# Local attention with whitening: second moments in two column halves, and every row point of the first image through the common path

## The chip, the core and the metric

The kernel runs on one core of one Trainium2 chip. The metric is device time in microseconds (us) of one execution. Engines are called PE (the matmul array), DVE (vector), ACT (scalar), POOL (GpSimd) and SP (the queue that issues most DMAs).

## What is computed

`x` has 4 images of 256 channels and 64 x 64 pixels. Layer 0 makes 49 attention weights per pixel and sums the 49 shifted neighbours with them; layer 1 whitens the result in groups of 64 channels. Cut to what matters:

```python
# layer 0
k = conv(x, w1, padding=6, dilation=2) + b1      # 7 x 7, 256 -> 128 channels
k = conv1x1(k, w2) + b2                          # 128 -> 49
attn = softmax(k, axis=1)
out = sum over (u, v) in 7 x 7 of attn[7u+v] * shift(x, 2u, 2v)
# layer 1, for every group g of 64 channels, m = 4*64*64 pixels
xc = X - mean(X)
Sigma = 1e-5 * I + xc @ xc.T / m                 # 64 x 64 per group
P = five Newton steps towards Sigma^(-1/2), Sigma scaled by its trace
y = (P / sqrt(trace)) @ xc * weight + bias
```

Only the 64 x 64 blocks of second moments within a group are used, never those between groups.

## The kernel before

Everything is fp32. The 256 channels lie as two chunks (`NCC`, index `cc`) of 128 partitions; a chunk holds two channel groups of 64 (`GW`). Each image is kept as two slots, one for each row parity, and dilation 2 makes each parity of rows and columns a plain 7 x 7 problem.

**Weight products (lines 198 to 236).** The two convolutions are folded into one with 49 outputs: for each of the 49 taps and each chunk the tap's slice of `w1` is the stationary side (`w1_sb[cc][:, :, tap]`, a column step of 49 words), and `w2` is the moving side. The 7-tap convolution is evaluated at seven points (0, 1, -1, 2, -2, 1/2 and infinity, `EVAL`, with `INF` = 6), so the moving side `w2c` holds `w2` scaled for the points. Four taps (`s` = 0) or three (`s` = 1) accumulate in one PSUM tile, which ACT copies to `gr` (the five middle points), `gr0` (point 0) and `gr6` (infinity). The latter two live in `lgx`, which later holds the logits of images 1 to 3.

**Row points (lines 275 to 440, helpers `add`, `sub`, `madd` at 262 to 270).** An image goes through row points `br`, and each through three banks of column points (`BANKS`). `row_eval` combines four input rows into `rb`; for points 0 and infinity it is only two ACT copies. `weights` combines the products for a bank into `wr` tiles the first time and writes them to DRAM (`gd`); later images read them back over SP. `col_eval` makes the column points `xh` on DVE. `conv_bank` multiplies into PSUM `cv`, 49 columns in each half of the array for the two column parities; ACT copies to `pv`; `col_interp` and, after the last row point, `row_interp` turn points back into pixels on DVE. `conv_step(k, i)` issues the matmuls of row point k, bank i, and then prepares the same bank of row point k+1. The first image takes only five row points this way (`MID`); points 0 and infinity are computed by `direct` (line 508) from `x` itself with single tap columns: 84 products into PSUM tile `acc`, placed after row points 1, 2 and 3.

**Attention (lines 601 to 731).** `softmax` of one column parity (`pc`) and one half of the rows turns logits, normalises and writes weights to DRAM (`sd`, 4 DMAs a call for each row parity). `load_band` reads a diagonal band back into the one tile `band`, DVE transposes it (line 666), and `weighted_sum` multiplies it with turned pixels into PSUM `y` (line 712). There are four such quarter images for each image (`n` = 0 to 15), each as `first_half` and `second_half`. ACT stores `y` over the input slot.

**Second moments (lines 736 to 763).** `turn_y` transposes a piece of the result, ACT copies it to `yt` (3 buffers, set to 1 beforehand, so that the last column of each chunk stays 1 and gives the sums), and `moments` adds 128 x 129 products for both chunks to PSUM `sig`, eight pieces for each quarter. Pieces 4 to 7 are done in `finish`, when the next quarter begins.

**Order of the work.** PE keeps the program's order. While row points of image b+1 are computed, pieces of image b's attention are called in eight gaps of that loop: `plan(b, j, ...)` puts work in gap j of image b, gaps from 8 on going to the next image. The softmax of an image takes gaps 0 and 1 of the next. Images 0 and 1 have their halves from gap 2 on, two at a time; images 2 and 3 have one half in each gap from gap 3 on. What is left over after the last convolution runs in a tail. After it `finish`, the 64 x 64 Newton steps (lines 899 to 962) and the output.

Of the kernel before, what the change touches and what calls it, by code (L numbers as in the profile page):

```python
# [30 lines left out]
def kernel(  # L31
# [134 lines left out]
    for k in range(2):  # L166
        t = ps_cv.tile([P, 512], F32, name=f"cv{k}")
        nc.vector.memset(t, 0.0)
        cv_buf.append(t)
    sig = ps_sg.tile([P, NCC, P + 1], F32, name="sig")  # L170

# [9 lines left out]
    w2c = w1p.tile([O1, 4, NP, KT], F32, name="w2c")  # L181

    def load_w1(cc):
        nc.sync.dma_start(
# [2 lines left out]
        )  # L187

    load_w1(0)
    load_w1(1)  # L190
    load_x(0, 0, nc.sync)
    load_x(1, 1, nc.sync)
    for cc in range(NCC):
        cs = slice(cc * P, (cc + 1) * P)
        nc.sync.dma_start(gain_sb[:, cc : cc + 1], gain[0, cs].rearrange("c a b -> c (a b)"))
        nc.sync.dma_start(shift_sb[:, cc : cc + 1], shift[0, cs].rearrange("c a b -> c (a b)"))

    WCOL = (INF,) + tuple(range(1, NP - 1)) + (0,)
    for a in range(4):
        for k, b in enumerate(WCOL):  # L200
            f = EVAL[b][a] * SCALE[b]
            if f:
                nc.vector.tensor_scalar(w2c[:, a, k], w2T[:, :KT], f, None, ALU.mult)
            elif (a, b) == (0, INF):
                nc.vector.memset(w2c[:, a, k], 0.0)


    n0, n6 = KS * NCC * 2 * KT, KS * NCC * KT
    lgx = const.tile([P, max(SH * W, n0 + n6)], F32, name="lgx")
    gr0 = lgx[:, :n0].rearrange("p (v a s k) -> p v a s k", v=KS, a=NCC, s=2)  # L210
    gr6 = lgx[:, n0 : n0 + n6].rearrange("p (v a k) -> p v a k", v=KS, a=NCC)

    for cc in range(NCC):
        for v in range(KS):
            for s in range(2):
                t = tp()
                na = min(4, KS - 4 * s)
                for a in range(na):
                    k0 = 0 if a == 3 or (a == 0 and s == 0) else 1
                    k1 = NP if a == 0 else NP - 1  # L220
                    pe(
                        nc.tensor.matmul(  # L222
                            t[:, k0 * KT : k1 * KT],
                            w1_sb[cc][:, :, (KS - 1 - 4 * s - a) * KS + v],
                            w2c[:, a, k0:k1].rearrange("p b k -> p (b k)"),
                            start=(a == 0), stop=(a == na - 1),
                        )
                    )
                nc.scalar.copy(
                    gr[:, :, v, cc, s],  # L230
                    t[:, KT : (NP - 1) * KT].rearrange("p (b k) -> p b k", b=MID),
                )
                nc.scalar.copy(gr0[:, v, cc, s], t[:, (NP - 1) * KT : NP * KT])
                if s == 0:
                    nc.scalar.copy(gr6[:, v, cc], t[:, :KT])
    w1p.release()

    s24 = ctx.enter_context(tc.tile_pool(name="s24", bufs=1, reuse_waits="tile"))
# [31 lines left out]
        return STT(o, a, f, b, ALU.mult, ALU.add)  # L270


    made = set()

    def weights(b, br, i):

        first = (br, i) not in made
        made.add((br, i))
        w = {}
        for bc in BANKS[i]:
            w[bc] = apool.tile(
                [P, len(taps(bc)), nsk[br]], F32, tag="wr", name=f"wr_{b}_{br}_{bc}", bufs=7
            )
            if not first:
                nc.sync.dma_start(w[bc], gd[br][:, slot_of[bc] : slot_of[bc] + len(taps(bc))])
        if not first:  # L290
            return w

        if br == INF:
# [186 lines left out]
    def row_interp(b):  # L480

        pt = {k: zz[:K2, k] for k in range(NP)}
        lg = lgx
        if b == 0:
            lg = store[4].rearrange("p c r w -> p (c r w)")
        lg = lg[:, : SH * W].rearrange("p (r w) -> p r w", w=W)
# [4 lines left out]
        logits[b] = lg  # L491

    logits = {}

    def direct(br, s):


        a = 3 if br == INF else 0
        if s == 0:
            acc[0] = ps_y.tile([P, 2, Q8, W], F32, tag="y", name=f"acc{br}")  # L500
            nc.vector.memset(acc[0], 0.0)  # L501
        ps = acc[0][:, s]
        order = [(v, cc) for v in sorted(range(KS), key=lambda v: abs(v - R)) for cc in range(NCC)]
        for j, (v, cc) in enumerate(order):
            d = 2 * (v - R)
            w0, w1_ = max(0, -d), min(W, W - d)
            for h in range(2):
                xs = slots[h].rearrange("p c (q a) w -> p a q c w", a=4)
                pe(
                    nc.tensor.matmul(  # L510
                        ps[h * HB : h * HB + KT, :, w0:w1_],
                        gr6[:, v, cc] if br == INF else gr0[:, v, cc, s],
                        xs[:, a, :, cc, w0 + d : w1_ + d],
                        start=(j == 0),
                        stop=(j == len(order) - 1),
                        skip_group_check=True,
                    )
                )
        z = zz[:K2, br]
        if s == 0:  # L520
            nc.scalar.copy(z[:, :Q8], ps[:K2])
            if br == INF:
                nc.vector.memset(z[:, Q8], 0.0)
        else:
            nc.scalar.copy(z[:, Q8], ps[:K2, Q8 - 1])
            add(z[:, 1:Q8], z[:, 1:Q8], ps[:K2, : Q8 - 1])

    acc = [None]
    rows = [(0, br) for br in ROWS if br not in (0, INF)]
    rows += [(b, br) for b in range(1, B) for br in ROWS]  # L530
    cur, nxt = {}, {}

    def prepare(k, i):
# [19 lines left out]
                row_interp(b)  # L553


    for k in range(MID):
        for i in range(len(BANKS)):
            conv_step(k, i)
        if 1 <= k < 4:
            direct(*((INF, 0), (0, 0), (0, 1))[k - 1])  # L560
        if k == 1:
            for s in range(2, 4):
                load_x(s, s, nc.gpsimd)
    gpool.release()

# [16 lines left out]
    NY = 3  # L582
    yt_buf = []
    for k in range(NY):
        a = bpool.tile([P, NCC, P + 1], F32, name=f"yt{k}")
        nc.gpsimd.memset(a, 1.0)
        yt_buf.append(a)
    sd = []
# [11 lines left out]

    def softmax(b, pc, hf):

        lv = logits[b].rearrange("p r w -> p (r w)")
        lt = tp().rearrange("p (i h k) -> p i h k", i=NI, h=2)
        for i in range(NI):
            pe(
# [129 lines left out]
    def turn_y(n, i):  # L736
        yt, pc = where(n)
        t = tp()
        for cc in range(NCC):
            pe(  # L740
                nc.tensor.transpose(  # L741
                    t[:, cc * P : (cc + 1) * P],
                    yt[:, cc, CR * i : CR * (i + 1), bass.ds(pc, SW, 2)],
                    ident,
                )
            )
        yb = ybs[n, i] = yt_buf[len(ybs) % NY]
        nc.scalar.copy(yb[:, :, :P], t[:, :C].rearrange("p (a c) -> p a c", a=NCC))  # L748

    def moments(n, i):  # L750
        yb = ybs[n, i]
        for cc in range(NCC):
            pe(
                nc.tensor.matmul(  # L754
                    sig[:, cc],
                    yb[:, cc, :P],
                    yb[:, cc, :],
                    start=(count[0] == 0 and cc == 0),
                    stop=(count[0] == 4 * B * NCH - 1),
                    skip_group_check=True,  # L760
                )
            )
        count[0] += 1

    spill = {}
# [87 lines left out]
    for b in range(B):  # L853
        hs = [
            (lambda n=n, f=f: f(n))
            for n in range(4 * b, 4 * b + 4)
            for f in (first_half, second_half)
        ]
        if b + 2 < B:

            plan(b + 1, 2, *hs[:2])
            plan(b + 1, 3, *hs[2:4])
            plan(b + 1, 4, finish)
            for j in range(4):
                plan(b + 1, 5 + j, hs[4 + j])
        else:
            for j in range(8):
                plan(b + 1, 3 + j, hs[j])
    for b in range(B):
        for j in range(2):  # L870
            plan(b + 1, j, lambda b=b, j=j: soft(b, j))
    plan(1, 1, lambda: load_x(4, 4, nc.gpsimd))

    def gap(b, j):
        for f in todo.pop((b, j), ()):
# [2 lines left out]
    for b in range(1, B):  # L878
        j = 0
        for q in range(nb):  # L880
            conv_step(MID + NP * (b - 1) + q // len(BANKS), q % len(BANKS))
            if (q + 1) * NPC >= (j + 1) * nb:
                gap(b, j)
                j += 1
# [15 lines left out]
    for cc in range(NCC):  # L900
        G = sig[:, cc]
        mu = work.tile([P, 1], F32, tag="mu", name=f"mu{cc}")
        nc.vector.tensor_scalar(mu, G[:, P : P + 1], 1.0 / NPIX, None, ALU.mult)
# [124 lines left out]
```

## Time and profile before

| | us |
|---|---|
| runs of the kernel | 983.78, 984.85, 984.92; median 984.85 |
| profiled execution, own time | 984.85 |
| its span, first to last instruction | 983.1 |
| busy PE, PE weight loads, DVE, ACT, POOL | 786.6, 666.2, 640.7, 298.3, 38.1 |
| weight products | 12.1 to 61.7 |
| first image up to the first weighted sum | 61.7 to 267.7 |
| rest of the loops, to the last convolution | 267.7 to 711.4 |
| tail with image 3's attention | 711.4 to 881.6 |
| Newton steps, then output | 881.6 to 920.5, to 983.1 |

The page of a profile gives busy time for each engine, the span in 40 slices with the busy tenths of each, the chain of work that ended last, and groups of instructions by line: count, busy time, mean duration of one in ns, the idle time of the engine just before them and what ended it. A group's busy time is a union, so overlapping matmuls count once. PE's own row and its weight loads (PEld) are separate; every fp32 product appears as two records of each. A duration contains latency: how fast a run of equal instructions goes is read from start to start in the timeline. A tile name stands for all of its buffers.

### The profile page before, as it was taken

The page shows a single profiled execution, that of the slowest core. Times are in us where ns is not written, and L with a number is a line of the kernel's source. Part 1 is how long each engine was busy: PE and PEld are TensorE (multiplying, and loading weights), DVE is VectorE, ACT ScalarE, POOL GpSimd, SP SyncE. Part 2 cuts the span into 40 slices and gives each one's busy share as a digit, 9 for nine tenths or more (in the row PEclk, how much of TensorE's full clock was granted, in tenths as well). Part 3 has the DMA queues.
Part 4 walks back from the last instruction along what each step waited for, and adds up shares of the span by engine and source line. Part 5 has one row for each costly group of instructions (what it writes and reads, how often), then busy time and mean ns, then how long its engine had stood idle before and what let it go on. Part 6 is the DMA issues. An engine that isn't in the chain of part 4 may idle for free.

```text
span 983.1 us, 18542 instructions
## 1 busy us (share of the span) xinstructions
PE 786.6 (80%) x7511; PEld 666.2 (68%) x7511; DVE 640.7 (65%) x1414; ACT 298.3 (30%) x677; POOL 38.1 (4%) x50
## 2 busy tenths in 40 slices
PE   5969829916699998958999896699983678786898
PEld 4968606816598897957898796598972557663443
DVE  2249997797968859994996799995572111113344
ACT  1333222321133343422434342133341323330143
POOL 2120001200000100010010000000000000000000
PEclk9989959958799999988999998799986979995699
DMA  8944111607762822598183239623219712100277
GB/s 303 203 102 149 55 53 55 232 29 159 146 129 60 246 67 67 168 198 165 39 242 97 53 88 163 146 55 77 61 63 268 131 42 48 44 1 0 88 309 287
DMA packets 187693, 120.10 MB, mean 122 GB/s; under 512 B 139303, under 2 KB 178648, under 8 KB 186584
## 3 DMA queue, kind: packets, MB, share of 16 engines
q1 hardware_dynamic: 182584, 88.77, 36.2%
q0 software_dynamic: 5024, 30.15, 10.0%
q8 instruction: 59, 0.97, 0.4%
q14 instruction: 26, 0.21, 0.1%
HBM read 67.68 MB, written 51.21 MB: 121 GB/s over the span
## 4 chain that ended last, share of the span: by engine, by line
PE 54%; DVE 16%; SPq 5%; DMA 4%; ACT 3%; issue 3%; DVEq 0%; ACTq 0%
PE cv L422 19%; PE y L712 15%; PE tp L974 6%; SPq L643 5%; PE sig L754 4%; PE acc L510 2%; PE tp L680 2%; DVE pv L270 2%; PE tp L741 2%; DMA band<-sd 2%; DVE xh L270 2%; DMA sd<-zt 2%; DVE band L666 1%; ACT slot L726 1%; DVE ct L270 1%
## 5 line engine op out<-in xcount | busy, mean ns | idle before, releaser
L422 PE MATMUL cv<-xh,wr 128*49 128x128 f32 (+1 forms) x5096 | 310.1, 284 | 31.0 <-issue 15.5
L422 PEld LDWEIGHTS cv<-xh,wr 128*49 128x49 f32 x5096 | 300.5, 126 | 39.1 <-issue 26.9
L712 PE MATMUL y<-band,xb 128*128 128x352 f32 (+5 forms) x768 | 177.9, 374 | 67.0 <-DVE band L666 53.9
L712 PEld LDWEIGHTS y<-band,xb 128*128 128x128 f32 x768 | 124.0, 205 | 87.5 <-issue 57.7
L666 DVE STREAM_TRANSPOSE band<-band 128x1408 f32<-128x1408 f32 x32 | 50.6, 1619 | 84.7 <-DMA band<-sd 84.7
L754 PE MATMUL sig<-yt 128*128 128x129 f32 x512 | 82.3, 283 | 16.5 <-ACT yt L748 16.5
L687 ACT COPY xb<-tp 128x256 f32<-128x256 f32 x128 | 45.7, 373 | 140.5 <-PE tp L680 140.3
L754 PEld LDWEIGHTS sig<-yt 128*128 128x128 f32 x512 | 71.2, 195 | 22.7 <-ACT yt L748 19.9
L431 ACT COPY pv<-cv 113x486 f32<-113x486 f32 (+1 forms) x78 | 36.7, 473 | 111.0 <-PE cv L422 110.8
L741 PE MATMUL tp<-ident,slot 128*128 128x128 f32 x256 | 53.5, 301 | 10.7 <-ACT slot L726 9.8
L726 ACT ACTIVATE slot<-y,pivot 128x512 f32<-128x512 f32 x64 | 42.5, 719 | 61.5 <-PE y L712 61.5
L748 ACT COPY yt<-tp 128x256 f32<-128x256 f32 x128 | 45.1, 376 | 34.2 <-PE tp L741 33.7
L222 PE MATMUL tp<-w2c,w 128*128 128x245 f32 (+2 forms) x196 | 49.6, 418 | 7.2 <-DMA w<-in_L_conv_w_dram 7.2
L222 PEld LDWEIGHTS tp<-w2c,w 128*128 128x128 f32 x196 | 47.8, 306 | 8.8 <-issue 8.2
L270 DVE SCALAR_TENSOR_TENSOR xh<-ct 128x512 f32<-128x512 f32 x52 | 34.1, 684 | 28.5 <-PE cv L422 28.5
L680 PEld LDWEIGHTS tp<-ident,slot 128*128 128x128 f32 x256 | 43.9, 204 | 12.5 <-issue 6.8
L510 PE MATMUL acc<-slot,lgx 128*49 128x496 f32 (+3 forms) x168 | 36.0, 587 | 20.2 <-DVE acc L501 20.2
L741 PEld LDWEIGHTS tp<-ident,slot 128*128 128x128 f32 x256 | 39.6, 204 | 18.5 <-ACT slot L726 15.1
L680 PE MATMUL tp<-ident,slot 128*128 128x128 f32 x256 | 51.8, 298 | 0.0
L989 DVE TENSOR_SCALAR out<-tp,scale,beta 128x512 f32<-128x512 f32 x32 | 25.9, 809 | 32.4 <-PE tp L974 32.4
L270 DVE SCALAR_TENSOR_TENSOR pv<-pv 113x162 f32<-113x162 f32 x156 | 45.6, 319 | 0.1
L270 DVE SCALAR_TENSOR_TENSOR xh<-rb 128x512 f32<-128x512 f32 x26 | 17.8, 686 | 35.4 <-PE cv L422 35.4
(166 smaller groups left out, 893.0 us busy)
## 6 DMA issues: line engine op xcount, KB each, us to landing
wr<-gd SPq DMA_DIRECT2D x102, 196.0 KB, 2.8
out_dram<-out SPq DMA_DIRECT2D x32, 512.0 KB, 2.6
sd<-zt SPq DMA_DIRECT2D x128, 112.0 KB, 3.0
band<-sd SPq DMA_DIRECT2D x64, 224.0 KB, 4.3
slot<-in_x_dram POOLq DMA_DIRECT2D x12, 1024.0 KB, 10.4
gd<-wr SPq DMA_DIRECT2D x36, 196.0 KB, 2.1
w<-in_L_conv_w_dram SPq DMA_DIRECT2D x2, 3136.0 KB, 15.0
spill<-slot POOLq DMA_DIRECT2D x3, 2048.0 KB, 9.5
```

The source lines that it names most:

```text
L222: nc.tensor.matmul(t[:, k0 * KT : k1 * KT], w1_sb[cc][:, :, (KS - 1 - 4 * s - a) * KS + v], w2c[:, a, k0:k1].rearrange("p b k -> p (b k)") ...
L270: return STT(o, a, f, b, ALU.mult, ALU.add)
L422: nc.tensor.matmul(cv[h * HB : h * HB + KT, k, sr : sr + n, sc : sc + n], wv[:, sc, sr, cc], xh[bc][:, :n, h * NCC + cc, :n], start=(j == ...
L510: nc.tensor.matmul(ps[h * HB : h * HB + KT, :, w0:w1_], gr6[:, v, cc] if br == INF else gr0[:, v, cc, s], xs[:, a, :, cc, w0 + d : w1_ + d ...
L643: nc.sync.dma_start(bass.AP(tensor=D.tensor, offset=D.offset + CR * (NI * hf + i) * DR + (KS - 1) * SW, ap=[[DQ, P], [DR - SW, KS], [1, SW ...
L666: nc.vector.transpose(f, f)
L680: nc.tensor.transpose(t[:, cc * P : (cc + 1) * P], xt[:, cc, CR * m : CR * (m + 1), bass.ds(pc, SW, 2)], ident,)
L712: nc.tensor.matmul(ps[:, cc, q0 - half * HALF : q1 - half * HALF, :], xb[:, cc * P : (cc + 1) * P], rhs, start=(k == 0), stop=(k == len(PI ...
L726: nc.scalar.activation(yt[:, cc, half * HALF : (half + 1) * HALF, bass.ds(pc, SW, 2)], ps[:, cc], AF.Identity, bias=pivot[:, cc : cc + 1],)
L741: nc.tensor.transpose(t[:, cc * P : (cc + 1) * P], yt[:, cc, CR * i : CR * (i + 1), bass.ds(pc, SW, 2)], ident,)
L754: nc.tensor.matmul(sig[:, cc], yb[:, cc, :P], yb[:, cc, :], start=(count[0] == 0 and cc == 0), stop=(count[0] == 4 * B * NCH - 1), skip_gr ...
L974: nc.tensor.matmul(t, wm[cc], slots[2 * b + pr][:, cc, q * TR : (q + 1) * TR, :].rearrange("p r w -> p (r w)"), start=True, stop=True,)
```

## The change

- `sig` shrinks from 129 to 65 columns for each chunk. `moments` issues, for each chunk, one product for each channel group: 64 stationary columns, 65 moving ones (64 channels and the ones), into the group's 64 partitions of `sig`, that is, into one half of the array's columns. `yt` has a ones column after each 64 channels.
- The Newton part clears `S` and scales the two diagonal blocks into it.
- `direct` is gone. The first image takes all seven row points in the common order (infinity, 0, 1, -1, 2, -2, 1/2), and its logits go to `lgx` like those of the others, so slot 4 is free from the beginning and is loaded with slots 2 and 3.
- Weight products: the five middle points (`middle`, 245 moving columns) and the end points (`ends`, single taps with `w2`, 49 moving columns, seven of them in one PSUM tile and one ACT copy) are separate, in the order ends, middle, ends, middle. `x`'s first slot is loaded ahead of the second chunk of `w1`.
- Halves of images 2 and 3 are planned from gap 2 instead of gap 3.

```diff
-    sig = ps_sg.tile([P, NCC, P + 1], F32, name="sig")
+    sig = ps_sg.tile([P, NCC, GW + 1], F32, name="sig")
...
     load_w1(0)
+    load_x(0, 0, nc.sync)
     load_w1(1)
-    load_x(0, 0, nc.sync)
     load_x(1, 1, nc.sync)
...
+    def tap(cc, a, s, v):
+        return w1_sb[cc][:, :, (KS - 1 - 4 * s - a) * KS + v]
+
+    def ends(cc):
+        for dst, a, s in ((gr6[:, :, cc], 3, 0), (gr0[:, :, cc, 0], 0, 0), (gr0[:, :, cc, 1], 0, 1)):
+            t = tp()
+            for v in range(KS):
+                pe(
+                    nc.tensor.matmul(
+                        t[:, v * KT : (v + 1) * KT], tap(cc, a, s, v), w2T[:, :KT],
+                        start=True, stop=True,
+                    )
+                )
+            nc.scalar.copy(dst, t[:, : KS * KT].rearrange("p (v k) -> p v k", v=KS))
...
-                    k0 = 0 if a == 3 or (a == 0 and s == 0) else 1
-                    k1 = NP if a == 0 else NP - 1
                     pe(
                         nc.tensor.matmul(
-                            t[:, k0 * KT : k1 * KT],
-                            w1_sb[cc][:, :, (KS - 1 - 4 * s - a) * KS + v],
-                            w2c[:, a, k0:k1].rearrange("p b k -> p (b k)"),
+                            t[:, : MID * KT], tap(cc, a, s, v),
+                            w2c[:, a].rearrange("p b k -> p (b k)"),
                             start=(a == 0), stop=(a == na - 1),
                         )
                     )
...
-                nc.scalar.copy(gr0[:, v, cc, s], t[:, (NP - 1) * KT : NP * KT])
-                if s == 0:
-                    nc.scalar.copy(gr6[:, v, cc], t[:, :KT])
+    ends(0)
+    middle(0)
+    ends(1)
+    middle(1)
...
-    rows = [(0, br) for br in ROWS if br not in (0, INF)]
-    rows += [(b, br) for b in range(1, B) for br in ROWS]
+    rows = [(b, br) for b in range(B) for br in ROWS]
...
-    for k in range(MID):
+    for k in range(NP):
         for i in range(len(BANKS)):
             conv_step(k, i)
-        if 1 <= k < 4:
-            direct(*((INF, 0), (0, 0), (0, 1))[k - 1])
         if k == 1:
-            for s in range(2, 4):
+            for s in range(2, 5):
                 load_x(s, s, nc.gpsimd)
...
-        a = bpool.tile([P, NCC, P + 1], F32, name=f"yt{k}")
+        a = bpool.tile([P, NCC, P // GW, GW + 1], F32, name=f"yt{k}")
...
-            pe(
-                nc.tensor.matmul(
-                    sig[:, cc],
-                    yb[:, cc, :P],
-                    yb[:, cc, :],
-                    start=(count[0] == 0 and cc == 0),
-                    stop=(count[0] == 4 * B * NCH - 1),
-                    skip_group_check=True,
+            for g in range(P // GW):
+                pe(
+                    nc.tensor.matmul(
+                        sig[g * GW : (g + 1) * GW, cc],
+                        yb[:, cc, g, :GW],
+                        yb[:, cc, g],
+                        start=(count[0] == 0 and cc == 0),
+                        stop=(count[0] == 4 * B * NCH - 1),
+                        skip_group_check=True,
+                    )
                 )
-            )
...
-                plan(b + 1, 3 + j, hs[j])
+                plan(b + 1, 2 + j, hs[j])
...
-    plan(1, 1, lambda: load_x(4, 4, nc.gpsimd))
...
-        nc.vector.tensor_scalar(S, G[:, :P], 1.0 / NPIX, None, ALU.mult)
+        nc.vector.memset(S, 0.0)
+        for g in range(P // GW):
+            gs = slice(g * GW, (g + 1) * GW)
+            nc.vector.tensor_scalar(S[gs, gs], G[gs, :GW], 1.0 / NPIX, None, ALU.mult)
```

More of the change, by code (lines that the diff above doesn't have):

```diff
@@ L180 @@
     w1_sb = [w1p.tile([O1, P, KT], F32, name=f"w1_{cc}") for cc in range(NCC)]
-    w2c = w1p.tile([O1, 4, NP, KT], F32, name="w2c")
+    w2c = w1p.tile([O1, 4, MID, KT], F32, name="w2c")
     def load_w1(cc):
@@ L196, with middle @@
         nc.sync.dma_start(shift_sb[:, cc : cc + 1], shift[0, cs].rearrange("c a b -> c (a b)"))
-    WCOL = (INF,) + tuple(range(1, NP - 1)) + (0,)
     for a in range(4):
[L200 to L205, printed above, removed]
+        for b in range(1, NP - 1):
+            nc.vector.tensor_scalar(
+                w2c[:, a, b - 1], w2T[:, :KT], EVAL[b][a] * SCALE[b], None, ALU.mult
+            )
     n0, n6 = KS * NCC * 2 * KT, KS * NCC * KT
     lgx = const.tile([P, max(SH * W, n0 + n6)], F32, name="lgx")
+    lg = lgx[:, : SH * W].rearrange("p (r w) -> p r w", w=W)
     gr0 = lgx[:, :n0].rearrange("p (v a s k) -> p v a s k", v=KS, a=NCC, s=2)
     gr6 = lgx[:, n0 : n0 + n6].rearrange("p (v a k) -> p v a k", v=KS, a=NCC)
-    for cc in range(NCC):
+    def tap(cc, a, s, v):
[11 more added lines that the diff above has]
+            nc.scalar.copy(dst, t[:, : KS * KT].rearrange("p (v k) -> p v k", v=KS))
+    def middle(cc):
         for v in range(KS):
@@ L230 @@
                     gr[:, :, v, cc, s],
-                    t[:, KT : (NP - 1) * KT].rearrange("p (b k) -> p b k", b=MID),
+                    t[:, : MID * KT].rearrange("p (b k) -> p b k", b=MID),
                 )
-                nc.scalar.copy(gr0[:, v, cc, s], t[:, (NP - 1) * KT : NP * KT])
-                if s == 0:
-                    nc.scalar.copy(gr6[:, v, cc], t[:, :KT])
+    ends(0)
+    middle(0)
+    ends(1)
+    middle(1)
     w1p.release()
@@ L270, in madd @@
         return STT(o, a, f, b, ALU.mult, ALU.add)
-    made = set()
     def weights(b, br, i):
-        first = (br, i) not in made
-        made.add((br, i))
         w = {}
@@ L287, in weights @@
             )
-            if not first:
+            if b:
                 nc.sync.dma_start(w[bc], gd[br][:, slot_of[bc] : slot_of[bc] + len(taps(bc))])
-        if not first:
+        if b:
             return w
@@ L482, in row_interp @@
         pt = {k: zz[:K2, k] for k in range(NP)}
[L483 to L486, printed above, removed]
         outs = [t[:, 0] for t in phases(lg[:K2].unsqueeze(1))]
@@ L490, in row_interp @@
         nc.scalar.activation(f, f, AF.Identity, bias=bias[:K2])
[L491 to L508, printed above, removed]
-                pe(
[L510 to L515, printed above, removed]
-                        skip_group_check=True,
-                    )
[L518 to L528, printed above, removed]
-    rows = [(0, br) for br in ROWS if br not in (0, INF)]
-    rows += [(b, br) for b in range(1, B) for br in ROWS]
+    rows = [(b, br) for b in range(B) for br in ROWS]
     cur, nxt = {}, {}
@@ L601, in softmax @@
     def softmax(b, pc, hf):
-        lv = logits[b].rearrange("p r w -> p (r w)")
+        lv = lg.rearrange("p r w -> p (r w)")
         lt = tp().rearrange("p (i h k) -> p i h k", i=NI, h=2)
@@ L747, in turn_y @@
         yb = ybs[n, i] = yt_buf[len(ybs) % NY]
-        nc.scalar.copy(yb[:, :, :P], t[:, :C].rearrange("p (a c) -> p a c", a=NCC))
+        nc.scalar.copy(
+            yb.rearrange("p a g c -> p (a g) c")[:, :, :GW],
+            t[:, :C].rearrange("p (e c) -> p e c", c=GW),
+        )
     def moments(n, i):
@@ L752, in moments @@
         for cc in range(NCC):
-            pe(
-                nc.tensor.matmul(
-                    sig[:, cc],
-                    yb[:, cc, :P],
-                    yb[:, cc, :],
-                    start=(count[0] == 0 and cc == 0),
-                    stop=(count[0] == 4 * B * NCH - 1),
-                    skip_group_check=True,
+            for g in range(P // GW):
[7 more added lines that the diff above has]
+                        skip_group_check=True,
+                    )
                 )
-            )
         count[0] += 1
@@ L880 @@
         for q in range(nb):
-            conv_step(MID + NP * (b - 1) + q // len(BANKS), q % len(BANKS))
+            conv_step(NP * b + q // len(BANKS), q % len(BANKS))
             if (q + 1) * NPC >= (j + 1) * nb:
@@ L902 @@
         mu = work.tile([P, 1], F32, tag="mu", name=f"mu{cc}")
-        nc.vector.tensor_scalar(mu, G[:, P : P + 1], 1.0 / NPIX, None, ALU.mult)
+        nc.vector.tensor_scalar(mu, G[:, GW : GW + 1], 1.0 / NPIX, None, ALU.mult)
         t = tp()
```

## The prediction

> **What bounds the kernel now.** I read the page's slices first, to see which engine is full where.
>
> ```profile
> PE   5969829916699998958999896699983678786898
> DVE  2249997797968859994996799995572111113344
> ```
>
> A slice is 24.6 us. TensorE (PE) is full in slices 2 and 3 and again from about 270 to 735 us; VectorE (DVE) is full from 60 to 260 us, where PE is not. After 735 us neither is full. So there are four stages with different limits, and the sums by stretch say how long each is:
>
> ```profile
> 12.10:61.70 49.60, 49.58 (x196) 47.77 (x196) 6.17 (x7) 14.04 (x68) 3.54 (x2) 1.00 0.83 185
> 61.70:267.70 206.00, 137.10 (x1720) 111.30 (x1719) 185.21 (x451) 55.53 (x122) 15.72 (x17) 0.83 0.41 115
> 711.40:791.50 80.10, 46.57 (x272) 39.54 (x271) 33.16 (x64) 23.38 (x55) 1.61 (x3) 0.80 0.61 148
> ```
>
> Columns: stretch, length, busy PE, weight loads, DVE, ScalarE (ACT), GpSimd, clock, DMA. Weight products: PE never stops. First image up to the first weighted sum (267.7): DVE works 185.2 of 206.0 us, so 20.8 us are its idle time. After the last convolution (711.4) until image 3's first weighted sum (791.5): 80.1 us in which everybody waits. Third, the rows of the lines concerned:
>
> ```profile
> L754 PE MATMUL sig<-yt 128*128 128x129 f32 x512 | 82.3, 283 | 16.5 <-ACT yt L748 16.5
> L222 PE MATMUL tp<-w2c,w 128*128 128x245 f32 (+2 forms) x196 | 49.6, 418 | 7.2 <-DMA w<-in_L_conv_w_dram 7.2
> L222 PEld LDWEIGHTS tp<-w2c,w 128*128 128x128 f32 x196 | 47.8, 306 | 8.8 <-issue 8.2
> L754 PEld LDWEIGHTS sig<-yt 128*128 128x128 f32 x512 | 71.2, 195 | 22.7 <-ACT yt L748 19.9
> L510 PE MATMUL acc<-slot,lgx 128*49 128x496 f32 (+3 forms) x168 | 36.0, 587 | 20.2 <-DVE acc L501 20.2
> ```
>
> Every fp32 product is two records. A load of 128 columns lasts 306 ns from `w1_sb` (column step 49 words) and 195 ns from packed tiles: 111 ns more.
>
> **Where the moments stand.** The timeline of PE, twice within full-width work, then at both edges of half-width work (`cv`, 49 columns in each half):
>
> ```profile
> 297.63 0.40 PE L741 MATMUL tp<-ident,slot 128*128 128x128 f32 x2
> 297.87 0.61 PE L754 MATMUL sig<-yt 128*128 128x129 f32 x4
> 298.32 0.40 PE L741 MATMUL tp<-ident,slot 128*128 128x128 f32 x2
> ```
>
> ```profile
> 294.61 0.98 PE L422 MATMUL cv<-xh,wr 128*49 128x162 f32 x14
> 295.51 0.39 PE L741 MATMUL tp<-ident,slot 128*128 128x128 f32 x1
> 295.74 0.52 PE L741 MATMUL tp<-ident,slot 128*128 128x128 f32 x3
> ...
> 313.86 0.61 PE L754 MATMUL sig<-yt 128*128 128x129 f32 x4
> 314.40 0.35 PE L422 MATMUL cv<-xh,wr 128*49 128x162 f32 x2
> ```
>
> A chunk's moments hold PE 0.45 us (297.87 to 298.32), between transposes. Before half-width work they hold it 0.54 us: entering costs 0.09, and by the trace's start times the first pair of `cv` then takes 0.176 us where later ones of its width take 0.14, its load being in the open: 0.04 more. Leaving: seven pairs from 294.61 (one of 0.14, six of 0.108) end at 295.40, but the next start is 295.51 and the one after comes 0.23 later, not 0.12: 0.10 + 0.10 us.
>
> **What the Trainium skill says.** "TensorEngine Tiling (Array Packing)", Key Properties: changing the tiling mode drains the array; the trace agrees, 0.09 and 0.10 us at the two edges. "TensorE: Matmul & The Clock Gate", section LDWEIGHTS: a load takes its columns divided by 1.2 ns; 107 for 128 columns, and the trace has the next load 111 ns later where the moving side is only 64 or 96 wide. For 64 columns it gives 53 ns. "SBUF — State Buffer", the note on 16-byte lines: a step over 4 fp32 words pays at each line; the 306 against 195 ns agree. The same TensorE page calls ACT and DVE strict FIFO, used in 2.
>
> **The change, part by part** (against the profiled execution: 984.85 us, span 983.1; it is also the median of the runs).
>
> *1. Weight products.* Before: 98 products with 245 to 343 moving columns, 49.6 us. After: 98 with 245 and 42 with 49, so 196 + 84 loads. Where several 245-wide records follow each other now, their start times grow apart from 206 to 220 ns and stay there, although 245 columns stream in about 204: the loads bound them (111 + the 111 extra = 222). A 49-wide record hides no more. 280 x 0.220 = 61.6 us from 12.1 on: end at 73.7 + 0.3. Cost 74.0 - 61.7 = **+12.3**. Bounds: 0.111 per end load and 0.207 per middle one, +0.4; 0.308 per end load (no overlap), +19. w1's second half now lands after x, at some 30 us by the rate of 327 GB/s in the first 20 us; it is needed after 140 records, at 43: free, with 13 us to spare; beyond that PE would wait the excess, with all later products behind it.
>
> *2. First image.* It loses 84 direct products and gains two row points of the common path. PE: 36.0 us go, 312 records at 0.056 = 17.5 come, all beside DVE. DVE pays: two column evaluations (2 steps of 1.13 and 7 of 0.60 each: 13.0), two column interpolations (19 of 0.24, 3 of 0.22: 10.4), the second pair of row-1 sums, formerly done under the products (2.3); off go a memset and an addition (1.5) and seven small INF weight steps now done under the products (1.2). 185.2 + 23.0 = 208.2. The weight steps of points INF and 0 only move within this stretch. Idle: between 152.3 and 187.2 DVE idles 12.1 us beside the direct products, which goes. It waits 6.5 us for `sd<-zt` while slot 4's load (issued at 234.5) shares the DMA; that load moves to the start of the image, later such waits are about 2.5, so 4 go. New: in ACT's order the two row copies of INF stand behind the last weight copy, so DVE waits 0.4 + 2 x 1.0, and 0.9 for INF's last bank. 20.8 - 12.1 - 4 + 3.3 = 8.0. 216.2 - 206.0 = **+10.2**; if only half the idle goes +18, if more overlaps at the seam +5. The 14 extra weight reads on SP (2.8 us to landing) come two rows later and lie under DVE's 7 us of column work a row; uncovered, a read would hold its bank's matmuls those 2.8 us.
>
> *3. Moments.* Four pairs of 65 columns: loads 53, stream 54, so I take 0.058 a pair, 0.232. Between full-width work a chunk pays 0.09 + 0.05 (64-column load) to enter and 0.20 to leave. 0.232 + 0.34 - 0.45 = +0.12 to +0.13. Ten chunks stand directly ahead of `cv` and save about 0.2; three adjoin another chunk. The order of the built program has 278 width changes for 46. On the path are some 85 of 128: images 0 and 1 up to the next softmax 24 each, image 2 20, the last four 17; the others lie under waits for the band. 72 x 0.13 - 13 x 0.2 = **+7**. Bounds: pairs as slow as loads in turn (0.112) +25; load hidden on leaving and entering, -4. ACT's copy keeps its 256 elements; the final halves cost two more short DVE steps, 0.1.
>
> *4. Plan one gap earlier for images 2 and 3.* In the last loop PE will wait for the first band as it did one image earlier (soft transposes at 401.4, sum at 444.1: 42.7 us). From 578.6 that is 621.3, against 640.9 now, with 208 `cv` records (11.9) still to do: 4 us ahead at the same point. Behind that wait on PE stand the sums of the half and the row points after it; DVE, which has kept PE waiting there, works on under it. One more half (finish 4, sums 5.6) is done in the loop: the convolutions end 5.6 later. Then the chain:
>
> ```profile
> 741.67 8.26 SPq L643
> 749.97 4.55 SPq L643
> ...
> 770.16 0.58 DVE zt L634
> ...
> 775.16 3.08 DMA sd<-zt
> ...
> 785.28 4.35 DMA band<-sd
> 789.75 1.66 DVE band L666
> ```
>
> The first writes to `sd` hold SP 13 us while the three 2 MB returns that GpSimd issued at 731.5 fill the DMA; that stays. From 770 on it is the second column parity's softmax that goes ahead of the band; in the built order of SP that band now precedes these writes. 783.8 - 769.5 = 14.3 us leave the 80.1. 5.6 - 14.3 = **-8.7**. If the band gains nothing, +5.6.
>
> Sum: 12.3 + 10.2 + 7 - 8.7 = +20.8; 984.85 + 20.8 = 1005.7.
>
> **Rivals.** *A, halves in turn* (the split doesn't overlap): pairs at 0.112 add 0.216 x 85 = 18: 1024. Against it: `cv`'s two loads start 7 ns apart and neither lasts longer than the other. *B, no gain from the plan*: +14: 1020; for it, the returns stay in the queue ahead of the first writes. *C, end loads hidden at the packed rate*: -12: 994; against it the 220 ns. *D, free switching*, ending on the other side: if changes of width cost nothing for these short products, 85 chunks save 0.218 each, -18.5 for +7: 980. It makes the kernel faster only if entering and leaving together cost under some 0.05 us a chunk; the edges above show 0.33. It is the only case I give below 984.85.
>
> **Chances.** Forecast 0.60, A 0.11, B 0.13, C 0.10, D 0.06. Some 2 us (0.2%) is what a measurement of this kernel can tell from no change; within it lies 0.02 of C and D. Faster 0.05, within 0.02, slower 0.93. From C's 994 to A's 1024 leaves out D and the outer halves of A and C, under 0.2; the forecast alone is 998 to 1015.
>
> **What would show it.** Products ending at 74 us (1); the first weighted sum near 290 with no direct products and DVE nearly unbroken (2); a moments group of eight records at 0.23 us with 0.1 us gaps on both sides (3); image 3's first sum 66 us after the last convolution (4). Products done by 62, or pairs 0.11 apart, or no gaps, would make the number wrong.

## The result and the profile after

The changed kernel takes 995.79 us (median of 4 runs, 995.47 to 996.29), the kernel before 984.32 (4 runs, 983.44 to 984.92): ratio 1.0118, 95% interval 1.0100 to 1.0135. That is 11.5 us slower; forecast were 20.8. The direction held, and so did three of the four steps within 3.3 us each; the fourth, the gain of the moved plan, was put at less than half of what it is.

The slices of DVE in the changed kernel, to be laid beside those of before (a slice is now 24.9 us):

```profile
DVE  3007999999995876999488599979467311124344
```

DVE now stands at 9 without a break from slice 5 to slice 12 (99 to 298 us), where before it had three sevens, two of them beside the direct products, and a six; from the second image on the pictures are alike. The sums by stretch (columns as in the prediction: stretch, length, busy PE, weight loads, DVE, ACT, POOL, clock, DMA) for the same three stages:

```profile
12.00:77.20 65.20, 65.17 (x280) 63.62 (x280) 3.97 (x11) 12.60 (x33) 3.53 (x2) 0.95 0.62 144
77.20:290.10 212.90, 128.98 (x1862) 124.88 (x1862) 207.74 (x506) 63.72 (x134) 15.71 (x17) 0.81 0.42 117
744.10:799.10 55.00, 35.76 (x281) 27.55 (x277) 29.69 (x61) 19.34 (x44) 1.62 (x3) 0.83 0.74 192
```

Cut at the same events in both traces, the whole span reads so (us; the last column is the forecast, with its +7 for the moments spread over the stretches by its count of pieces, 24, 24, 20 and 17):

| up to | before | after | difference | forecast |
|---|---|---|---|---|
| end of the weight products (from 0) | 61.7 | 77.2 | +15.5 | +12.3 |
| image 0's first weighted sum | 206.0 | 212.9 | +6.9 | +10.2 |
| image 1's first softmax | 133.7 | 136.7 | +3.0 | +2.0 |
| image 2's first softmax | 177.2 | 179.8 | +2.6 | +2.0 |
| the last convolution | 132.8 | 137.5 | +4.7 | +5.6 and +1.6 |
| image 3's first weighted sum | 80.1 | 55.0 | -25.1 | -14.3 |
| end of attention | 90.1 | 93.9 | +3.8 | +1.4 |
| end (Newton steps and output) | 101.5 | 101.5 | 0 | 0 |

The first two lines give +22.4 where +22.5 was forecast, but by two errors that cancel. The large miss is the tail. This is the row of the changed moments:

```profile
L722 PE MATMUL sig<-yt 128*64 128x65 f32 x1024 | 58.2, 235 | 9.4 <-ACT yt L712 8.9
```

The moments' busy time falls from 82.3 to 58.2 us, and this is no gain of 24 us: what the change of width costs lies in the gaps between groups, which no row counts. The timeline of PE shows it:

```profile
301.05 0.39 PE L644 MATMUL tp<-ident,slot 128*128 128x128 f32 x2
301.37 0.45 PE L722 MATMUL sig<-yt 128*64 128x65 f32 x8
301.76 0.51 PE L705 MATMUL tp<-ident,slot 128*128 128x128 f32 x2
302.10 1.16 PE L676 MATMUL y<-band,xb 128*128 128x64 f32 x8
```

From start to start: 0.32 us from the two transposes to the moments, where two transposes took 0.24 before; 0.39 to the next transposes; 0.34 for these, 0.24 before. The eight records themselves start within 0.23 us. Together 1.05 us where it was 0.93: the forecast 0.12 to 0.13 for a piece between full-width work.

### The profile page after: what moved, and what is told of

It is laid out like the page before. It is cut to its first block, busy times and chain, and to the rows that moved or that the text cites. A ratio compares the mean times of both kernels' runs of the same rounds, so it can differ in the third digit from the quotient of the medians.

```text
span 994.5 us, 20076 instructions
## 1 busy us (share of the span) xinstructions
PE 801.3 (81%) x8251; PEld 677.6 (68%) x8251; DVE 661.4 (67%) x1473; ACT 305.3 (31%) x654; POOL 38.1 (4%) x50
## 4 chain that ended last, share of the span: by engine, by line
PE 52%; DVE 9%; ACT 4%; DMA 3%; SPq 3%; issue 3%; DVEq 0%; ACTq 0%
PE cv L430 19%; PE y L676 16%; PE tp L944 6%; PE sig L722 3%; PE tp L705 3%; SPq L607 3%; PE tp L644 2%; DMA band<-sd 2%; DVE band L630 1%; ACT slot L690 1%; ACT pv L439 1%; DVE pv L282 1%; DMA sd<-zt 1%; DVE zz L282 1%; DVE xh L282 1%
## 5 line engine op out<-in xcount | busy, mean ns | idle before, releaser
L430 PE MATMUL cv<-xh,wr 128*49 128x128 f32 (+1 forms) x5408 | 334.3, 286 | 59.7 <-DVE xh L275 49.7
L430 PEld LDWEIGHTS cv<-xh,wr 128*49 128x49 f32 x5408 | 324.3, 128 | 65.9 <-issue 61.1
L676 PE MATMUL y<-band,xb 128*128 128x352 f32 (+5 forms) x768 | 183.1, 382 | 64.7 <-DVE band L630 47.2
L676 PEld LDWEIGHTS y<-band,xb 128*128 128x128 f32 x768 | 125.7, 207 | 86.6 <-DVE band L630 37.1
L439 ACT COPY pv<-cv 113x486 f32<-113x486 f32 (+1 forms) x84 | 39.9, 474 | 106.5 <-PE cv L430 106.2
L705 PE MATMUL tp<-ident,slot 128*128 128x128 f32 x256 | 59.2, 324 | 10.2 <-ACT slot L690 9.3
L722 PE MATMUL sig<-yt 128*64 128x65 f32 x1024 | 58.2, 235 | 9.4 <-ACT yt L712 8.9
L722 PEld LDWEIGHTS sig<-yt 128*64 128x64 f32 x1024 | 40.4, 137 | 33.7 <-ACT yt L712 13.2
L644 PE MATMUL tp<-ident,slot 128*128 128x128 f32 x256 | 55.5, 314 | 0.0
L644 PEld LDWEIGHTS tp<-ident,slot 128*128 128x128 f32 x256 | 44.1, 206 | 15.8 <-issue 8.0
L275 DVE TENSOR_TENSOR ct<-rb 128x1024 f32<-128x1024 f32 x28 | 33.9, 1210 | 28.6 <-ACT rb L361 28.4
L282 DVE SCALAR_TENSOR_TENSOR pv<-pv 113x162 f32<-113x162 f32 x168 | 48.9, 318 | 0.1
L233 PE MATMUL tp<-w2c,w 128*128 128x245 f32 x196 | 47.1, 406 | 0.0
```

The lines of the kernel that those rows point to most:

```text
L233: nc.tensor.matmul(t[:, : MID * KT], tap(cc, a, s, v), w2c[:, a].rearrange("p b k -> p (b k)"), start=(a == 0), stop=(a == na - 1),)
L430: nc.tensor.matmul(cv[h * HB : h * HB + KT, k, sr : sr + n, sc : sc + n], wv[:, sc, sr, cc], xh[bc][:, :n, h * NCC + cc, :n], start=(j == ...
L439: nc.scalar.copy(pvs[b, br][:K2, i0 : i0 + len(pts)].rearrange("p n q b -> p (n q b)"), cv[:K2, : len(pts)].rearrange("p n q b two -> p (n ...
L644: nc.tensor.transpose(t[:, cc * P : (cc + 1) * P], xt[:, cc, CR * m : CR * (m + 1), bass.ds(pc, SW, 2)], ident,)
L676: nc.tensor.matmul(ps[:, cc, q0 - half * HALF : q1 - half * HALF, :], xb[:, cc * P : (cc + 1) * P], rhs, start=(k == 0), stop=(k == len(PI ...
L705: nc.tensor.transpose(t[:, cc * P : (cc + 1) * P], yt[:, cc, CR * i : CR * (i + 1), bass.ds(pc, SW, 2)], ident,)
```

## Experiments

The theory going in: four separate terms, at the sizes of the table. The rival to all of them: the terms need each other, that is, the shorter tail is slack which the later start creates, and the growth between 290 and 607 us is a lower clock. The first four kernels each make one part of the change on the kernel before.

**Moments alone** (`b_mom`): the edits to `sig`, `yt`, `moments` and `S`, nothing else.

> The kernel before with only the moments changed to four products of 64 x 65 per chunk. Theory (each lone group of narrow products costs 0.12 to 0.13 us more than the wide ones, because array mode changes and an uncovered load cost 0.34 us and the products save only 0.22): +7 as forecast; +11 if all of the growth seen in the stages from 290 to 607 us and after 799 us is theirs. Rival (changes of mode are nearly free, and the growth of those stages is the lower granted clock or the moved plan): between -18 and +2.

989.63 us against 984.57: ratio 1.0050 (1.0037 to 1.0064), so +3.6 to +6.3. The forecast +7 lies just outside. At the measured 0.12 us a piece +4.9 means a net 40 pieces on the path; +7 had been 72 that cost less 13 that save, a net 54 at 0.13. Free changes of mode (-18) are excluded.

**Plan alone** (`b_plan`).

```diff
-                plan(b + 1, 3 + j, hs[j])
+                plan(b + 1, 2 + j, hs[j])
```

> The kernel before with only the plan of images 2 and 3 moved one gap ahead. Theory (the writes of weights in the tail no longer meet the three returns in the DMA, on top of the second parity's softmax leaving the path): -19 to -23. Rival 1, as forecast (the returns still hold the first writes by 13 us): -8.7. Rival 2 (part of the shorter tail is slack that the later products and first image create, so it needs them): between -8 and 0.

965.50 us: ratio 0.9802 (0.9789 to 0.9816), -18 to -21. The sums of image 2 begin at 622.6 (forecast 621.3) and the convolutions end at 716.9 against 711.4 (+5.5, forecast +5.6). The tail needs nothing else from the change, and is as short here as in the changed kernel:

```profile
716.90:772.20 55.30, 34.79 (x215) 29.73 (x213) 29.72 (x61) 19.07 (x44) 1.62 (x3) 0.83 0.73 190
```

So the rival that it is slack from the later start falls, and so does the forecast's -8.7; the theory's -19 to -23 holds. Everything the plan costs in the loop was forecast; what it gives in the tail was not.

**Weight products alone** (`b_prod`): `ends` and `middle` in place of the combined products, and the order of the two loads; `direct` stays.

> The kernel before with only the weight products separated (ends, middle, ends, middle) and x's first slot loaded ahead of the second half of w1; the direct products stay. Theory (every record waits for its strided load of 0.22 us, 84 records more): +12 to +15 at the end. Rival (later stages absorb part, as DVE or DMA waits there shrink): +0 to +8.

1002.65 us: ratio 1.0183 (1.0162 to 1.0205), +16 to +20. In its trace the products end at 77.5 (+15.8) and the stretch after them is 205.6 us, as before: nothing absorbs it. The whole is above both expectations: 2 us beyond the products' own 15.8 are not placed (the traced run is the slowest of the four, and in it the stretches after the first image are 5.6 us longer).

**First image alone** (`b_rows`): no `direct`, seven row points, slot 4 early; products combined as before.

> The kernel before with only the first image changed: no direct products, all seven row points in common, slot 4 loaded early; products combined as before. Theory: +7 (stage seen in the changed kernel) to +10 (forecast), all of it DVE work. Rival (the direct products were hidden nowhere and PE sets that stage: the 36 us they held PE go, 17.5 come): -5 to 0.

995.41 us: ratio 1.0109 (1.0095 to 1.0123), +9.4 to +12.1. The stretch after the products is 214.6 us (+8.6), with DVE busy 209.5 of it; PE's 36 us of direct products had been hidden.

The four alone add up to +5.1 - 19.1 + 18.1 + 10.8 = +14.9, the whole change to +11.5. The intervals (about 3 us for the sum, 1.7 for the whole) leave open whether 3 us are given back somewhere.

**What an end product costs** (`a_pack`, on the changed kernel):

```diff
-                        t[:, v * KT : (v + 1) * KT], tap(cc, a, s, v), w2T[:, :KT],
+                        t[:, v * KT : (v + 1) * KT],
+                        w1_sb[cc].rearrange("o c t -> o (c t)")[:, v * P : (v + 1) * P],
+                        w2T[:, :KT],
```

> The changed kernel, with the stationary side of the end products taken from 128 neighbouring words instead of a tap's words 49 apart; so the end points get other weights, and their part of the computation is not the reference's. Theory (each of the 168 end records is held by its strided load, 0.22 us against 0.11 for neighbouring words, in two runs of 42 loads each): 84 loads x 0.11 = 9 us off the products, 986 in all. Rival (a record of 49 columns costs 0.22 for another reason, such as the PSUM tile or the lower clock): 994 to 997.

991.36 us, ratio 1.0052 (1.0036 to 1.0069) to the kernel before, about 6 less than the changed kernel by the two ratios; in the trace the products end at 72.8, 4.4 us earlier, and the remaining 2 lie within the intervals. The time falls between the theory's 986 and the rival's 994. The 4.4 us are half of the 9 us that the theory asked for in the products, and the timeline of PE in this kernel says which half:

```profile
12.16 9.20 PE L219 MATMUL tp<-w2T,w 128*128 128x49 f32 x42 [7.43 <-DMA w<-in_L_conv_w_dram]
21.16 23.78 PE L235 MATMUL tp<-w2c,w 128*128 128x245 f32 x98
44.77 4.86 PE L219 MATMUL tp<-w2T,w 128*128 128x49 f32 x42
```

The second run of 42 falls from 9.0 us to 4.65 (start to start; 0.111 a record): there the strided load was the cost. The first run goes only from 9.2 to 9.0 (0.213 a record) although its loads are packed. 0.213 is about twice 0.111, and the records after it show the same halving. The stretches of the changed kernel just behind the second run of ends, and four us later:

```profile
54.10:56.10 2.00, 2.00 (x6) 1.72 (x7) 0.00 (x0) 0.45 (x1) 0.00 (x0) 0.50 1.01 213
58.10:60.10 2.00, 2.00 (x11) 2.00 (x11) 0.00 (x0) 0.37 (x1) 0.00 (x0) 1.00 0.05 10
```

Six records of 245 columns in 2 us at a granted clock of 0.50, then eleven at 1.00. By their starts, the first 12 middle records of the first chunk and the first 6 of the second are about 0.41 us apart, the others 0.22. (The view shows 1.00 at 21.2 to 23.2 too, with the same six records. The trace's clock entries begin only at 26.1, where the first 0.41 spacing ends; the view counts what lies ahead of them as 1.00.) The DMA is full in the first of these two stretches and nearly idle in the second, but it is not the reason. The same two microseconds in `a_pack` have it just as full and hold eleven records:

```profile
54.10:56.10 2.00, 2.00 (x11) 2.00 (x11) 0.00 (x0) 0.41 (x2) 0.00 (x0) 1.00 0.99 209
```

The kernel before begins at half clock as well, with its wide products:

```profile
14.10:16.10 2.00, 2.00 (x6) 1.48 (x6) 0.16 (x1) 0.00 (x0) 0.00 (x0) 1.00 1.00 414
```

Its first 13 records take 6.1 us, where 13 of the same forms later take 3.1, and its clock entries begin at 18.1, where that ends. So the first run of ends doesn't make the half clock, it leaves it standing: 6 us of wide products ended it before, 9.2 us of ends don't. The second run falls back to it; the entries show 0.50 from 50.0 to 56.8. The Trainium skill, "TensorE: Matmul & The Clock Gate", Part 1, says that half clock is the default and activity releases it. The trace fits that, if products that stream 49 columns in 220 ns count as too little activity; this cause is an inference with the page's help, and the runs show only the half clock through and behind the ends. 280 x 0.220 = 61.6, and 18 records x 0.19 = 3.4 more: 65.0 from 12.0 on, measured 65.2.

**Two pieces of moments at a time** (`b_wide2` as a control of the order, `b_mom2` with the narrow products). Both, on the kernel before, with the last two of a quarter treated alike:

```diff
         make_block(n, 7)
-        moments(n, 0)
         turn_y(n, 2)
         weighted_sum(n, 1, 1)
         make_block(n, 5)
+        moments(n, 0)
         moments(n, 1)
...
-        moments(n, 2)
         weighted_sum(n, 1, 4)
         store_y(n, 1)
+        moments(n, 2)
         moments(n, 3)
```

> The kernel before with the moments of two pieces issued directly after each other instead of one by one; still 128 x 129. A control for the order alone. Both theories: within 2 us of before, for the wide products change no array mode.

> Narrow moments as in the change, on the kernel before, but two pieces directly after each other, so half as many changes of array mode. Theory (0.34 us for each lone group, about 85 groups on the path, half of them gone, minus what the order alone does): 12 to 15 us less than the narrow moments one by one, so 7 to 10 us less than before. Rival (changes of mode are nearly free and the narrow moments lost time to the clock or to the order): within 2 us of the narrow ones one by one, so +3 to +7.

979.12 (ratio 0.9929, 0.9913 to 0.9946) and 976.40 (0.9900, 0.9874 to 0.9925), with 986.16 for the kernel before. Both expectations for the control were wrong: the order alone gives 7 us. Of 5.7 us by which its trace is shorter, 3.5 lie between image 3's first sum and the end of attention (86.6 us, 90.1 before), and the moments' waits for ACT's copy fall from 16.5 to 11.6 us in all; how much of that is the cause was not followed further. The narrow products' number is as expected, but only because of that. Against the right partner, narrow costs +0.5% one piece at a time and -0.3% two at a time (the second not separable from zero), a difference of about 8 us, where 14 were expected. With a net 40 pieces on the path the prices give 40 x (0.34 / 2 - 0.218) = -1.9 and a difference of 6.8. So the prices hold, the rival of free changes falls, and the count behind the 14 was the forecast's, too high.

**What holds the first writes in the tail.** Three kernels try to take the three returns away from the writes. `b_ret` moves their issue, on GpSimd, to the end of the program:

> The kernel before, with the three returns of 2 MB issued at the very end of the tail instead of at its beginning; nothing else moves. Theory (in the tail the returns hold up both the first eight writes of weights, 16 us where the changed kernel took 7, and the band load issued just before them, 18 us): 9 to 14 us less than before. Rival (the writes and the band are held by the order of SP's queue and by softmax, not by the returns): within 2 us of before.

985.42 against 986.16, ratio 0.9990 (0.9981 to 1.0000): nothing. But it tested nothing either, as the timeline of GpSimd in this kernel shows:

```profile
732.87 1.62 POOL L891 DMA_DIRECT2D back<-spill  x3 [222.83 <-ACT xb L687]
```

GpSimd has no other work there, so its next DMA starts as soon as what it waits for is there, wherever it stands in the program; in the kernel before it was 731.5. `b_ret2` therefore gives them to SP:

```diff
-        nc.gpsimd.dma_start(t.rearrange("p a r w -> p (a r w)"), spill[k])
+        nc.sync.dma_start(t.rearrange("p a r w -> p (a r w)"), spill[k])
```

> The kernel before, with the three returns issued by SP behind the last band of the tail, so that they can't start earlier (moved on GpSimd's own queue they had started at the same time as before, since that queue has nothing else to wait for). Theory (the returns fill the DMA while the last band of image 2 lands, 18 us, and while the first eight writes of weights are issued, 16 us): 9 to 14 us less than before. Rival (SP's order and softmax hold them): within 2 us of before.

980.48 against 985.12, ratio 0.9961 (0.9947 to 0.9974): -3 to -5, between the two expectations. The returns did not go last here either: in the built order SP issues them one by one between the groups of writes.

```profile
733.86 0.34 SPq L891 DMA_DIRECT2D back<-spill  x1
...
742.91 7.09 SPq L643 DMA_DIRECT2D sd<-zt  x8
750.10 0.55 SPq L891 DMA_DIRECT2D back<-spill  x1
753.51 9.09 SPq L643 DMA_DIRECT2D sd<-zt  x8
762.69 0.54 SPq L891 DMA_DIRECT2D back<-spill  x1
766.34 8.10 SPq L643 DMA_DIRECT2D sd<-zt  x8
```

That makes it a measurement of doses. With one return 9 us ahead instead of three 10 us ahead, the first eight writes take 7.1 us instead of 16.7, and the sums that waited for image 2's last band begin at 749.2 instead of 757.3. But the second and third groups, now each some 3.5 us behind a return of their own, take 9.1 and 8.1 instead of 6.0 and 5.0. These two returns land at 759.7 and 771.7, and the longest single write of each group (3.7 and 3.3 us) ends at 760.0 and 771.9. The time moves with the returns: they are what holds the writes. How much their full removal would give wasn't reached.

`b_plan_ret2` makes the same edit with the moved plan:

> The same late returns, with the plan moved one gap ahead as in the change. Theory (the moved plan brings the first writes 14 us after the returns' start, when these have nearly passed; only one write of 3 us is still held): 0 to 4 us less than the moved plan alone, so 961 to 966. Rival (the returns cost as much here as in the kernel before): 952 to 957.

963.59, ratio 0.9786 (0.9774 to 0.9799), within 2 us of the plan alone. Again not what was meant: in this built order SP issued all three returns at 732.2, 14 us before the first write. So it says nothing about late returns.

**Putting together what helped.** `b_plan_mom2` takes the plan and the paired narrow moments; `b_all` adds the returns on SP and puts image 3's first softmax ahead of the seventh half of image 2.

> The plan moved one gap ahead together with narrow moments two pieces at a time, on the kernel before. Theory (both act in places of their own, so they add): 19 + 10 = 29 us less than before, 954 to 958. Rival (in the tail the shorter moments lie under the waits that the plan leaves): 960 to 964.

953.54, ratio 0.9687 (0.9668 to 0.9706), -29 to -33: the gains add.

> As the one before, with the late returns and with the first softmax of image 3 ahead of the seventh half of image 2 instead of behind it. Theory (with the moved plan the tail's chain is image 3's last logits, that half's sums, then softmax, writes, band; softmax need not wait for the sums): 8 us less for the order and 0 to 4 for the returns, so 943 to 950. Rival (the band of that half or DVE's transposes end last anyway): 953 to 958.

950.08, ratio 0.9647 (0.9630 to 0.9663): 35 us faster than the kernel before, but only about 4 less than the one above, where 8 to 12 were expected. The chain of waits in `b_all`:

```profile
725.95 1.78 PE tp L607 x8
...
732.27 0.37 ACT yt L748
732.65 0.44 ACT d L623
...
735.13 0.37 SPq L643
```

Softmax's transposes do come 5.7 us earlier than in `b_plan_mom2` (731.6 there), but ACT's exponential stands in ACT's order behind copies of turned results (`yt`), and the first write is issued at 735.1 instead of 736.8. With only two returns ahead of them the first eight writes then take 4.9 us and none is held; but SP issues the third return at 740.1, between the groups, and the second eight take 9.3. After sixteen writes the lead is 1.8 us (752.5 against 754.3).

## Why the prediction was right in direction and high by 9 us

*1. Weight products, +12.3: too small.* The price of 0.220 us a record held to the digit, in both runs of ends. The step took the clock for granted: "A 49-wide record hides no more" was right about the load, and nothing was said of half clock, neither of the 3 us of it in the 49.6 of before nor of what the ends would leave. 18 middle records at 0.41 us are the missing 3.2 us. `a_pack` adds that in the first run half clock alone would have held the records at 0.213, stride or not.

*2. First image, +10.2: right in kind.* DVE was forecast at 208.2 us and is busy 207.7. The idle time was forecast at 8.0 and is 5.2 (212.9 - 207.7), which is nearly the whole miss of 3.3. DVE's wait for `sd<-zt`, forecast to fall from 6.5 us to 2.5, is gone altogether; the longest waits left are 2.9 us in all for writes to `gd`. Made alone the step costs +8.6 in its stretch and +10.8 in all.

*3. Moments, +7: right in price, the count too high.* 0.058 us a pair, drained at both edges, 0.12 for a lone piece: all in the timeline. Alone it costs +5, so "On the path are some 85 of 128" was too many; which of them lie under other waits was not taken apart. In the changed kernel the stretches show +3.0, +2.6 and +3.8; how much of these is the clock (the kernel with only the products changed, whose moments are as before, also shows +2.6 in the second and +1.8 in the last of these stretches) stays open.

*4. Plan, -8.7: the step that failed.* Its loop half was exact (621.3 and +5.6 forecast, 622.6 and +5.5 measured). Its tail half said: "The first writes to `sd` hold SP 13 us while the three 2 MB returns that GpSimd issued at 731.5 fill the DMA; that stays." It did not stay. The chain of waits of the changed kernel, for the lines shown of before:

```profile
775.84 1.18 SPq L607
...
777.06 3.13 SPq L607
...
782.27 2.94 DMA sd<-zt
```

In place of 8.26 + 4.55 us the longest holds are 1.18 and 3.13; from the first write to the eighth it is 7.3 us, 16.0 before: 8.7 of the 10.8 missed. The returns in both traces, before and after, each with the times of all three from issue to landing (the last issued is the last to land):

```profile
L889 POOL DMA_DIRECT2D back<-spill x3: 528/547/558, 731.5 to 732.6; - x3
DMA to landing us min/median/max: 8.6/13.8/20.2
...
L856 POOL DMA_DIRECT2D back<-spill x3: 531/547/558, 761.3 to 762.4; - x3
DMA to landing us min/median/max: 8.4/12.7/17.5
```

They were issued 9.8 us ahead of the first write before and 13.6 ahead now (761.3 to 774.9). So the last one landed at 752.8, 11.4 us after the first write, and lands now at 779.9, 5.0 us after it. The long hold ends at 754.5 and at 780.2, behind that landing in both. It does so in all eleven traces in which GpSimd issues the three returns: the hold ends 0.2 to 1.8 us after the last of them has landed. With `b_ret2` this shows that their landing is what frees the writes. They moved because softmax of image 3 now stands in the tail behind a half that waits for its band behind DVE's last logits; in the step I had moved the writes and the band and left the returns where they stood, relative to them. The other part, the second parity's softmax leaving the chain ahead of the band, was forecast at 14.3 and is 16.8 (766.9 to 783.8 before, nothing now): +2.5.

Added up in the trace: products 3.2 over the forecast, first image 3.3 under, tail 10.8 under, moments and loop together 1.5 over (14.1 against 7 + 5.6): -9.4, from +20.8 to +11.4. Of the rivals, halves in turn (0.112 a pair) and free switching fell to the timeline, packed loads to the 0.220, and no gain from the plan to `b_plan`. The likeliest case was the right one with its largest gain undersized. The number itself owes something to luck: the misses of the first two steps cancel, and 995.8 lies below the 998 to 1015 that I gave the forecast alone, beside the 994 of rival C, whose end loads at the packed rate the runs refute (0.22 us a record).

## What to carry to other kernels

A sum of parts is tested by making each part alone: here one of four carried a gain of 19 us under three that cost 34, and that one alone beats both kernels. When work moves past a bulk transfer, work out anew how long after the next small DMA that transfer will land; "that stays" is a claim with a number. And price a short matmul by its load, its edges and what it does to the clock, not by its busy time.

## What was not expected of the hardware

- PE was at half clock behind runs of 42 products with 49 moving columns: the next 6 to 12 products of 245 columns were 0.41 us apart instead of 0.22, with a granted clock of 0.50 where it was recorded. Both kernels began at half clock; wide products left it after 6 us, the ends did not in 9.2.
- In the first run, at half clock by the spacing behind it, the stride of the stationary side cost next to nothing (0.213 us packed, 0.220 at a step of 49 words); at full clock it doubled the record (0.219 against 0.111).
- Writes of 112 KB issued behind returns of 2 MB were held at their issue, and the hold ended 0.2 to 1.8 us after the last return had landed.
- DMAs moved down on GpSimd's queue, which had nothing else to do, started when they did before (732.9 against 731.5).
- Issuing wide moments in pairs rather than singly saved 7 us without a change of any operation.
